# Preparing the last attention's first pair inside the first attention, in a two-layer fp32 kernel on one core

## The chip, the cores and the metric

The kernel runs on one core of a Trainium2 chip. Its time is the device time of one execution in microseconds, and the median of three runs is taken. TensorE (PE) multiplies matrices, VectorE (DVE), ScalarE (ACT) and GpSimd (POOL) work on rows, SyncE (SP) issues most transfers. Each engine runs its own queue of instructions in order and waits on semaphores for the others.

## The reference

Four stages in turn are added to x, of 4 batches, 512 tokens and 256 channels, all in fp32:

```python
x = x + _L0_attn_ref(_layernorm(x, axis=-1), ...)   # linear attention
x = x + _L0_ffn_ref(_layernorm(x, axis=-1), ...)    # Hadamard FFN
x = x + _L1_attn_ref(_layernorm(x, axis=-1), ...)   # "first attention" below
x = x + _L1_ffn_ref(_layernorm(x, axis=-1), ...)    # "last attention" and experts
```

`_L1_attn_ref` is softmax attention over 16 query heads and 4 key/value heads of 16 channels, with rotated queries and keys. `_L1_ffn_ref` starts with another attention, causal, and ends with a mixture of experts:

```python
h = _rms(x, ln_w)
q = (h @ wq).reshape(B, S, NHEADS, HEAD_DIM)      # 32 heads of 64
k = (h @ wk).reshape(B, S, KVHEADS, HEAD_DIM)     # 8 heads
v = (h @ wv).reshape(B, S, KVHEADS, HEAD_DIM)
q, k = _rope(q, k)
...
x = x + o @ wo
h = _rms(x, ff_ln_w)
...
return x + moe
```

Here x enters already as a layer norm of the residual, so each token has two factors: `zinv`, the layer norm's inverse root of the variance, and `hinv`, that of the RMS norm on top of it, both worked out from the token's mean and variance `mvs`.

## The kernel before, in words

Tokens are cut in tiles of 128, four to a batch (`NT`); `xt[i]` holds one tile of the residual. The order of the instructions on each engine is written by hand (`manual_schedule`): the order of the Python calls is the order in the queues. Four stages follow each other: the linear attention, the FFN (which also makes keys and queries of the first attention for batches 0 and 1), the first attention, the last attention with routing and experts.

**The first attention** (from L940) is one loop of 66 steps, 16 to a batch: step `i` of batch `b` is head group `j = i // 4` and token tile `t = i % 4`. A step issues, in this order:

- `row_fill1` for the next batch: four score matmuls (L329) and four row maxima on DVE (L335). In batch 3 there is no next batch, so these are missing;
- at `i = 0`, `maxima1` (L977, L980) and `complete1`; at every other step one piece from the list `fill1` (`extra1`); at `t = 2` another `complete1` (POOL, L962, L965, L967), which makes the shifted query and key of the next head group;
- `normalise1` (ACT L1020 and L1021, four POOL operations L1022 to L1025) at `i = 2, 6, 10, 14`, for the head group finished before;
- `col_fill1`: four transposed score matmuls (L989) and four exponentials on ACT (L995);
- `weigh1` (L1002) for the step before and, after a group's last tile, `sums1` (ACT copy L1012, DVE shuffle L1014).

The pieces of `fill1` are queries and values of the next batch, the four token tiles of the previous batch's out-projection (`out_proj1`: eight matmuls of L234, the DVE add L1031 and the statistics L1033 and L1034, which fill `mvs`) from step 5, and `fresh1`, rows, transposes, keys and queries of the batch after next. PSUM is a ring of seven banks beside one for the weighed sums.

**The seam** between the two attentions: after the loop come the last `normalise1` and the four `out_proj1` of batch 3. Then `inv_root_log` works out the norms of all 16 token tiles at once, twice (L210 to L218, L1093 to L1098): a DVE scale and shift, Ln and Exp on ACT, one Newton step on DVE. With `zinv` and `hinv` there, `fresh(0)` normalises the rows of batch 0 (`norm_rows`, four POOL operations, L1149) and transposes them (`turn`, L1170; ACT leaves by L1176).

**The last attention** runs by pairs of units. A unit is eight query heads, made in two blocks of `q_lo` and `q_hi`, and two key/value heads; a pair of units shares `keys_lo`, `keys_hi` (both in `rope_half`: four matmuls L225, an ACT copy L1190, two POOL multiplications L1193 for a low half, four operations L1199 and L1200 for a high half) and `values` (L234, ACT copy L1251, eight transfers to DRAM L1257). `twice` copies keys to both halves of the partitions (SP, L1234), `spread` brings values back from DRAM in another layout (SP, L1271), and `normed` makes the rows `z` of the new residual (POOL, L1160). `q_hi` also orders the next query weights (`fetch_q`, SP, L1207). For the first pair all of that is issued ahead of the loop. Then a loop of five steps to a unit issues score fills (`fill`, L1298), DVE minima with the causal mask (`least`, L1316), exponentials (L1328), DVE transposes (L1345), weighing (L1375) and out-projections with `wo4` (L1425). In it a list `soon` holds work that is dealt out by the step, with "pause" entries that end a step's share. The weight `wo4` (2 MB) is loaded with the others ahead of the first attention.

Of the kernel before, what the change touches and what calls it, by code (L numbers as in the profile page):

```python
# [10 lines left out]
F32 = mybir.dt.float32  # L11
# [78 lines left out]
def kernel(  # L90
# [172 lines left out]
    def rows_of(b):  # L263
        tiles = []
        for t in range(NT):
            i = b * NT + t
            xn = piece_tile([P, D], "xn1", 4)
            nc.gpsimd.tensor_scalar(
                xn, xt[i], amv[:, i, 0:1], ainv[:, i : i + 1],
                ALU.subtract, ALU.mult,  # L270
            )
            tiles.append(xn)
        xnTs[b] = piece_tile([P, KC, S], "xnT1", 2)
        return tiles
# [63 lines left out]
    with ExitStack() as l0:  # L338
# [352 lines left out]
        with ExitStack() as f0:  # L691
# [5 lines left out]
            made1 = {}  # L697

            def outliving(shape, tag, bufs):
                if tag[:2] in ("qp", "kr", "kz"):  # L700
                    made1[tag] = made1.get(tag, -1) + 1
                    return wp5.tile(
                        shape, F32, tag=f"{tag}_{made1[tag]}", bufs=1, name=tag
                    )
                return fp.tile(shape, F32, tag=tag, bufs=bufs, name=tag)

            where["tile"] = outliving
# [180 lines left out]
    wo4 = wp4.tile([P, 16, D], F32, tag="wo4", name="wo4")  # L888
# [7 lines left out]
    nc.sync.dma_start(out=wo4, in_=w_o4)  # L896
# [38 lines left out]

    banks.close()
# [5 lines left out]
    with ExitStack() as a1:  # L942
        a1.enter_context(tc.manual_schedule())
        with tc.issue_after(latest["root"].ins):
# [7 lines left out]
        where["tile"] = lambda shape, tag, bufs: ap1.tile(  # L952
            shape, F32, tag=tag, bufs=bufs, name=tag
        )
# [96 lines left out]
        last = held = None  # L1051
        for k in range(4 * NT * B + 2):
# [4 lines left out]
            if i == 3 and 1 < b + 1 < B:  # L1057
                fill1.append(lambda b=b: values1(b + 1))
            if i == 5 and 0 < b <= B:
                fill1.extend([lambda t=t, b=b: out_proj1(b - 1, t) for t in range(NT)])  # L1060
            if i == 5 and b + 2 < B:
                fill1.extend(fresh1(b + 2))
            if b + 1 < B:
                row_fill1(b + 1, j, t)
# [7 lines left out]
            if held is not None:  # L1072
                normalise1(*held)
                held = None
# [5 lines left out]
            if last is not None:  # L1080
                weigh1(*last)
                if last[2] == NT - 1:
                    held = last[:2] + sums1(*last[:2])
            last = at + (pT,) if pT is not None else None
        normalise1(*held)
        assert not fill1
        for t in range(NT):
            out_proj1(B - 1, t)

        inv = inv_root_log(mvs[:, :, 1], EPS_LN, B * NT)
        nc.vector.tensor_copy(zinv, inv)  # L1093
        msq = stat.tile([P, B * NT], F32, tag="msq", name="msq")
        nc.vector.tensor_tensor(msq, zinv, zinv, ALU.mult)
        nc.vector.tensor_tensor(msq, msq, mvs[:, :, 1], ALU.mult)
        inv = inv_root_log(msq, EPS_RMS, B * NT)
        nc.vector.tensor_tensor(hinv, inv, zinv, ALU.mult)  # L1098
# [10 lines left out]
    with ExitStack() as a2:  # L1109
# [3 lines left out]
        units = []  # L1113
# [5 lines left out]

        def unit(name):  # L1120
            pool, bufs = units[-1]
            return pool.tile([P, 512], F32, tag="u", bufs=bufs, name=name)

        NU = 4 * B
        hTs, zs, krs, vsrs, qrs, lots, pend = ({} for _ in range(7))
        scores, probs, turned, heaps, wides, rsb, oTs, vds = ({} for _ in range(8))


        held = []
        putting_off = [False]  # L1130

        def drain(fn):
            if putting_off[0]:
                held.append(fn)
            else:
                fn()

        def drain_one():
            if held:
                held.pop(0)()  # L1140


        def norm_rows(b):
            hTs[b] = ap2.tile([P, KC, S], F32, tag="hT", bufs=2, name="hT")
            hn = []
            for t in range(NT):
                i = b * NT + t
                h = rp.tile([P, D], F32, tag="hn", bufs=4, name="hn")
                nc.gpsimd.tensor_scalar(  # L1149
                    h, xt[i], mvs[:, i, 0:1], hinv[:, i : i + 1],  # L1150
                    ALU.subtract, ALU.mult,
                )
                hn.append(h)
            return hn
# [9 lines left out]

        def turn(dst, col, srcs, scale):

            pt = unit("pt").rearrange("p (c n) -> p c n", c=KC)
            for i, src in enumerate(srcs):
                for c in range(KC):
                    nc.tensor.transpose(  # L1170
                        pt[:, c, i * P : (i + 1) * P], src[:, c * P : (c + 1) * P], ident
                    )

            def leave():
                for c in range(KC):
                    nc.scalar.activation(  # L1176
                        dst[:, c, col : col + 2 * P], pt[:, c, :], AF.Copy,
                        scale=scale[:, c : c + 1],
                    )

            drain(leave)

        def rope_half(dst, half, w, at, hT, scale):

            pr = unit("pr")
            project(pr, w, slice(at, at + P), hT, slice(0, S))

            def leave():
                raw = ap2.tile([P, S], F32, tag="raw4", bufs=2, name="raw4")
                nc.scalar.activation(raw, pr, AF.Copy, scale=scale)  # L1190
                if half == 0:
                    for i, name in enumerate(("cos4", "sin4")):
                        nc.gpsimd.tensor_tensor(dst[:, i, :], raw, R(name), ALU.mult)  # L1193
                    return
                for i, (name, op) in enumerate(
                    (("sin4", ALU.subtract), ("cos4", ALU.add))
                ):
                    part = ap2.tile([P, S], F32, tag="part4", bufs=1, name="part4")
                    nc.gpsimd.tensor_tensor(part, raw, R(name), ALU.mult)  # L1199
                    nc.gpsimd.tensor_tensor(dst[:, i, :], dst[:, i, :], part, op)  # L1200

            drain(leave)

        def fetch_q(k):
            if k < 2 * NU:
                wqs[k] = wp4.tile([P, KC, 2 * P], F32, tag="wq4", bufs=3, name="wq4")
                nc.sync.dma_start(out=wqs[k], in_=w_q4[k % 8])  # L1207

        def q_lo(k):
            if k >= 2 * NU:  # L1210
                return
            qrs[k] = ap2.tile([P, 2, S], F32, tag="qr4", bufs=4, name="qr4")
            rope_half(qrs[k], 0, wqs[k], 0, hTs[k // 8], 1.0)

        def q_hi(k):
            if k >= 2 * NU:
                return
            rope_half(qrs[k], 1, wqs.pop(k), P, hTs[k // 8], 1.0)
            fetch_q(k + 3)


        def keys_lo(q):
            pend[q] = ap2.tile([P, 2, S], F32, tag="krq", bufs=1, name="krq")
            rope_half(pend[q], 0, wk4, 256 * (q % 2), hTs[q // 2], -0.125)

        def keys_hi(q):
            rope_half(pend[q], 1, wk4, 256 * (q % 2) + P, hTs[q // 2], -0.125)

        def twice(u):

            kr = ap2.tile([P, 2, S], F32, tag="kr4", bufs=2, name="kr4")
            part = slice(64 * (u % 2), 64 * (u % 2) + 64)
            for i in range(2):
                nc.sync.dma_start(  # L1234
                    out=kr[64 * i : 64 * i + 64, :, :], in_=pend[u // 2][part, :, :]
                )
            krs[u] = kr

        def values(q, half):
            if half == 0:  # L1240
                pend["v"] = ap2.tile([P, NT, 256], F32, tag="vs4", bufs=1, name="vs4")
            pv = unit("pv4").rearrange("p (t n) -> p t n", t=2)
            for i in range(2):
                project_tok(
                    pv[:, i, :], hTs[q // 2], tok(2 * half + i), wv4,
                    slice(256 * (q % 2), 256 * (q % 2) + 256),
                )
            vs = pend["v"]

            def leave():  # L1250
                nc.scalar.copy(vs[:, 2 * half : 2 * half + 2, :], pv)  # L1251
                if half == 1:

                    vd = dram.tile([2, 32, 16, P], F32, tag="vd", bufs=2, name="vd")
                    for p2 in range(2):
                        for cc in range(4):
                            nc.sync.dma_start(  # L1257
                                out=vd[p2, :, cc:16:4, :],
                                in_=vs[rows(cc), :, P * p2 : P * p2 + P],
                            )  # L1260
# [993 lines left out]
```

## Time and profile before

| | us |
|---|---|
| median of three runs | 1767.79 (1761.07 to 1770.71) |
| the profiled execution | 1779.78 |
| its span | 1777.9 |
| busy in the span: PE | 1624.5 (91%) |
| DVE | 1002.4 (56%) |
| ACT | 825.5 (46%) |
| POOL | 894.5 (50%) |

The mean granted clock over the span is 0.966. Times in the text below are microseconds from the start of the span of this execution. The profile's groups give, for each line, the number of instructions, their mean duration, and what ended the idle time ahead of them; the records in time order give a start, a busy time, the engine, line and operation, the output and inputs with their shapes, and in brackets the idle time before and its releaser. The busy shares are means over stages with different limits, and the stages are read apart below.

### The profile page before, as it was taken

To read this page: it belongs to the slowest core of one execution; us is meant where nothing else is said; L and a number is where in the kernel's file an instruction comes from. 1 tells how busy PE (TensorE), PEld (TensorE's weight loads), DVE (VectorE), ACT (ScalarE), POOL (GpSimd) and SP (SyncE) were. 2 spreads that over 40 slices of the span, in tenths; PEclk is the share of its full clock that TensorE was granted. 3 is DMA by queue.
4 is the path that set the end of the run, shared out by engine and by line. 5 is a ranking of instruction groups with operands and counts; after the bars stand their busy time and mean duration, and the time that the engine had idled before them with its cause. 6 is when DMAs were issued, how large, how long until landed. Compare 5 with 4: busy or idle time off the path is not lost.

```text
span 1777.9 us, 42123 instructions
## 1 busy us (share of the span) xinstructions
PE 1624.5 (91%) x16100; PEld 950.4 (53%) x16100; DVE 1002.4 (56%) x3069; ACT 825.5 (46%) x2162; POOL 894.5 (50%) x914
## 2 busy tenths in 40 slices
PE   7999999999999986899999999999989868899993
PEld 4665554553334223466666666666666635455552
DVE  4547336556666412667766686668756924433333
ACT  4431122125655762566666665666556514233331
POOL 3224133225565545755466647794667244844442
PEclk9999999999999997899999999999999979899997
DMA  9992000020000001322222222322222037655556
GB/s 348 371 369 84 0 1 0 1 102 1 1 1 1 1 1 43 77 55 56 56 56 55 56 56 56 87 75 59 61 61 68 6 122 235 154 97 87 86 88 167
DMA packets 106934, 146.59 MB, mean 82 GB/s; under 512 B 11632, under 2 KB 86128, under 8 KB 106352
## 3 DMA queue, kind: packets, MB, share of 16 engines
q1 hardware_dynamic: 91856, 123.54, 22.9%
q0 software_dynamic: 14448, 19.80, 6.5%
q8 instruction: 131, 2.15, 0.5%
q14 instruction: 67, 0.55, 0.1%
q10 hardware_dynamic: 432, 0.55, 0.1%
HBM read 67.17 MB, written 68.29 MB: 76 GB/s over the span
## 4 chain that ended last, share of the span: by engine, by line
PE 41%; POOL 5%; issue 5%; ACT 5%; DVE 4%; DMA 1%; SPq 0%; another core or an unknown queue 0%; ACTq 0%; DVEq 0%; POOLq 0%
PE po L1375 9%; PE ph L1947 8%; PE sc L1298 6%; PE py L1425 5%; PE pr L225 4%; PE pyx L1947 3%; ACT masked L1328 2%; PE pq L1403 1%; POOL xs L1612 1%; POOL part L1199 1%; DVE masked L1316 1%; ACT raw L1190 1%; PE ptx L1983 1%; PE pa L2016 1%; POOL qr L1200 1%
## 5 line engine op out<-in xcount | busy, mean ns | idle before, releaser
L1328 ACT ACTIVATE masked<-masked,mx 128x256 f32<-128x256 f32 (+3 forms) x512 | 281.1, 553 | 4.8 <-DVE mx L1316 4.8
L1316 DVE CUSTOM_DVE_ANT_0 masked<-sc,cst 128x256 f32<-128x256 f32 (+3 forms) x512 | 214.0, 481 | 44.6 <-PE sc L1298 44.5
L1375 PE MATMUL po<-pT,vsr 32*64 32x128 f32 (+1 forms) x8064 | 198.1, 289 | 39.6 <-issue 24.9
L1375 PEld LDWEIGHTS po<-pT,vsr 32*64 32x64 f32 x8064 | 158.3, 132 | 90.0 <-issue 41.8
L1345 DVE STREAM_TRANSPOSE pT<-masked 128x512 f32<-128x512 f32 x256 | 168.5, 691 | 57.7 <-ACT masked L1328 57.2
L2029 POOL DMA_INDIRECT acc<-yx,goes x79 | 123.2, 1559 | 138.9 <-ACT yx L2028 101.4
L335 DVE TENSOR_REDUCE top<-sc 128x1 f32<-128x512 f32 x256 | 158.7, 682 | 56.3 <-PE sc L329 56.3
L1298 PE MATMUL sc<-kr,qr 32*128 32x128 f32 (+3 forms) x2048 | 173.9, 460 | 10.8 <-POOL qr L1200 3.7
L1947 PE MATMUL ph<-wall,hTx 128*128 x316 | 163.5, 641 | 11.6 <-DVE hTx L1985 6.9
L995 ACT ACTIVATE pT<-sT 128x512 f32<-128x512 f32 x256 | 131.5, 604 | 60.8 <-PE sT L989 60.6
L1434 POOL TENSOR_TENSOR z<-z,y 128x256 f32<-128x256 f32 x64 | 47.3, 740 | 195.9 <-ACT y L1433 195.8
L1415 DVE TENSOR_TENSOR oT<-po,rsb 128x128 f32<-128x128 f32 x256 | 61.3, 287 | 139.4 <-PE po L1375 127.1
L2009 DVE TENSOR_TENSOR ax<-ph,gx 128x256 f32<-128x256 f32 x79 | 33.6, 425 | 166.2 <-ACT gx L2007 154.7
L1425 PE MATMUL py<-wo,oT 128*128 128x256 f32 x512 | 123.7, 390 | 2.3 <-DVE oT L1415 1.6
L1199 POOL TENSOR_TENSOR part<-raw,rtab 128x512 f32<-128x512 f32 x80 | 102.5, 1281 | 43.1 <-ACT raw L1190 39.8
L1298 PEld LDWEIGHTS sc<-kr,qr 32*128 32x128 f32 x2048 | 90.5, 189 | 60.5 <-issue 29.0
L225 PE MATMUL pr<-hT,wq 128*128 128x512 f32 x256 | 122.0, 601 | 0.0
L225 PE MATMUL pgu<-xnT,wug 128*128 128x512 f32 x256 | 114.5, 598 | 1.5 <-DVE xnT L190 1.5
L989 PE MATMUL sT<-qr,km 32*128 32x512 f32 x512 | 108.1, 634 | 7.0 <-POOL km L967 2.8
L1425 PEld LDWEIGHTS py<-wo,oT 128*128 128x128 f32 x512 | 94.6, 192 | 31.2 <-DVE pT L1345 7.6
L1406 ACT COPY rsb<-pq 128x512 f32<-128x512 f32 x64 | 36.0, 587 | 134.8 <-PE pq L1403 129.7
L1947 PEld LDWEIGHTS ph<-wall,hTx 128*128 128x128 f32 x316 | 55.8, 196 | 79.1 <-issue 43.2
(301 smaller groups left out, 2884.9 us busy)
## 6 DMA issues: line engine op xcount, KB each, us to landing
xs<-zero SPq DMA_DIRECT2D x16, 2304.0 KB
vsr<-vd SPq DMA_DIRECT2D x256, 64.0 KB
wall<-in_w_exp_dram SPq DMA_DIRECT2D x16, 768.0 KB
xin<-xs SPq DMA_DIRECT2D x79, 144.0 KB
wq<-in_w_q_dram SPq DMA_DIRECT2D x33, 256.0 KB
kr<-krq SPq DMA_DIRECT2D x32, 256.0 KB
acc<-zero SPq DMA_DIRECT2D x2, 2176.0 KB
vd<-vs SPq DMA_DIRECT2D x64, 64.0 KB
```

The source lines that it names most:

```text
L225: nc.tensor.matmul(dst, lhsT=w[:, c, cols], rhs=srcT[:, c, tok], start=(c == 0), stop=(c == n - 1),)
L335: nc.vector.tensor_reduce(top[:, at : at + 1], sc, AX.X, ALU.max)
L995: nc.scalar.activation(pT[:, g, :], us[g], AF.Exp)
L1199: nc.gpsimd.tensor_tensor(part, raw, R(name), ALU.mult)
L1298: nc.tensor.matmul(scs[s][:, at : at + w], lhsT=qrs[2 * u + jj][rows(s), ab, tok(t)], rhs=krs[u][rows(s), ab, :w], start=(ab == 0), stop=( ...
L1316: nc.vector.tensor_tensor_reduce(masked[:, part], sc[:, part], C("cmask")[:, S - (t + 1) * P :], 1.0, 3e38, ALU.add, ALU.min, mx[:, t, i : ...
L1328: nc.scalar.activation(part, part, AF.Exp, bias=lots[u, "mx"][:, t, i : i + 1], scale=-1.0, accum_out=lots[u, "sm"][:, t, i : i + 1],)
L1345: nc.vector.transpose(dst[:, 2 * (f % 2) + s // 2, :], p)
L1375: nc.tensor.matmul(heaps[u, phase][a][64 * g : 64 * g + 64, first * P : last * P], lhsT=vsrs[u][rows(a), c, 64 * g : 64 * g + 64], rhs=src ...
L1425: nc.tensor.matmul(py[:, :D], lhsT=oT[:, j, :], rhs=wo4[:, 4 * (u % 4) + j, :], start=(j == 0), stop=(j == 3),)
L1947: ins = nc.tensor.matmul(out, lhsT=lhsT, rhs=wall[:, bass.ds(w_at[i] + at, n)], **kw)
L2029: nc.gpsimd.indirect_dma_start(out=accs[i % 2][:, :], out_offset=bass.IndirectOffsetOnAxis(ap=goes[:, i : i + 1], axis=0), in_=y[:, :], in ...
```

## The change

1. The helpers of the last attention (`unit`, `norm_rows`, `turn`, `rope_half`, `q_lo`, `q_hi`, `keys_lo`, `keys_hi`, `twice`, `values`) are defined ahead of the first attention, and their tiles come from a new pool `w_first` (transposed rows and query tiles alternate between it and the old pool).
2. `first_pair`, a list of ten pieces, holds what was the preparation of the first pair. Seven are put into `fill1` at step 1 of batch 3, ahead of the out-projection of batch 2, which so moves from steps 5 to 8 to steps 8 to 11. The other three run behind the last `normalise1`, ahead of batch 3's out-projection.
3. `inv_root_log` at the seam is replaced by `norms(b, n)`, three pieces for `n` batches from `b`. Batch 0's are put into `fill1` in batch 1 and come at its steps 13 to 15, batch 1's in batch 2 at steps 9 to 11, those of batches 2 and 3 together in `soon`, in the last attention's steps 1 to 3. `norm_rows(0)` runs at step 12 of batch 2.
4. `wo4` becomes a tile of the last attention's pool and is loaded behind the first unit's `spread`; `normed(0)` goes into `soon`, at step 0.
5. To make room, the transposed rows `xnT1` have one buffer in place of two, and queries and keys of the first attention share one ring from the FFN on (`place_in`).

The core of the diff:

```diff
+    def norms(b, n):
+        part = slice(b * NT, (b + n) * NT)
+        st = {}
+
+        def begin(var, eps):
+            st["v"] = stat.tile([P, n * NT], F32, tag="rn_v", name="rn_v")
+            nc.vector.tensor_scalar(st["v"], var, 1.0, eps, ALU.mult, ALU.add)
+            st["y"] = stat.tile([P, n * NT], F32, tag="rn_y", name="rn_y")
+            nc.scalar.activation(st["y"], st["v"], AF.Ln)
+            nc.scalar.activation(st["y"], st["y"], AF.Exp, scale=-0.5)
+
+        def end():
+            y, r = st["y"], stat.tile([P, n * NT], F32, tag="rn_r", name="rn_r")
+            nc.vector.tensor_tensor(r, y, y, ALU.mult)
+            nc.vector.tensor_tensor(r, r, st["v"], ALU.mult)
+            nc.vector.tensor_scalar(r, r, -0.5, 1.5, ALU.mult, ALU.add)
+            nc.vector.tensor_tensor(r, r, y, ALU.mult)
+            return r
+
+        def second():
+            nc.vector.tensor_copy(zinv[:, part], end())
+            msq = stat.tile([P, n * NT], F32, tag="rn_m", name="rn_m")
+            nc.vector.tensor_tensor(msq, zinv[:, part], zinv[:, part], ALU.mult)
+            nc.vector.tensor_tensor(msq, msq, mvs[:, part, 1], ALU.mult)
+            begin(msq, EPS_RMS)
+
+        return [
+            lambda: begin(mvs[:, part, 1], EPS_LN),
+            second,
+            lambda: nc.vector.tensor_tensor(hinv[:, part], end(), zinv[:, part], ALU.mult),
+        ]
...
+        first_pair = [
+            lambda: turn(hTs[0], 0, hn1[:2], SM("ln_w")),
+            lambda: turn(hTs[0], 2 * P, hn1[2:], SM("ln_w")),
+            lambda: keys_lo(0),
+            lambda: (keys_hi(0), twice(0), twice(1)),
+            lambda: q_lo(0),
+            lambda: q_hi(0),
+            lambda: q_lo(1),
+            lambda: q_hi(1),
+            lambda: values(0, 0),
+            lambda: values(0, 1),
+        ]
...
+            if i == 1 and b == B - 1:
+                fill1.extend(first_pair[:7])
             if i == 5 and 0 < b <= B:
                 fill1.extend([lambda t=t, b=b: out_proj1(b - 1, t) for t in range(NT)])
             if i == 5 and b + 2 < B:
                 fill1.extend(fresh1(b + 2))
+            if i == 5 and 0 < b < B - 1:
+                fill1.extend(norms(b - 1, 1))
+            if i == 12 and b == B - 2:
+                fill1.append(lambda: hn1.extend(norm_rows(0)))
...
+        for piece in first_pair[7:]:
+            piece()
         for t in range(NT):
             out_proj1(B - 1, t)
-
-        inv = inv_root_log(mvs[:, :, 1], EPS_LN, B * NT)
...
-        start = fresh(0)
-        for _, piece in start:
-            piece()
-        keys_lo(0)
...
-        for a in range(4):
-            spread(0, a)
-        normed(0)
+        for i in range(4):
+            spread(0, i)
+        nc.sync.dma_start(out=wo4, in_=w_o4)
+        soon.append((False, lambda: normed(0)))
+        for piece in norms(2, 2):
+            soon += [(False, piece), ("pause", lambda: None)]
```

## The prediction

> **What bounds the kernel now.** I read the busy time by stretches first, then the chain that ended last, then the records in time order around the place where the first attention gives way to the last one (the seam). By stretches; columns are length, busy PE, PEld, DVE, ACT, POOL (with instruction counts), granted clock, DMA share, GB/s:
>
> ```profile
> 603.00:659.00 56.00, 51.93 (x326) 16.63 (x326) 7.82 (x22) 43.64 (x85) 32.28 (x29) 1.00 0.00 1
> 659.00:704.00 45.00, 28.81 (x84) 17.47 (x88) 7.33 (x28) 7.37 (x16) 21.96 (x19) 0.81 0.10 23
> 704.00:745.00 41.00, 32.34 (x391) 15.69 (x383) 25.14 (x88) 24.83 (x77) 35.65 (x29) 0.83 0.35 84
> ...
> 790.00:834.00 44.00, 41.52 (x753) 27.29 (x743) 30.43 (x109) 26.69 (x82) 27.94 (x25) 1.00 0.23 61
> ```
>
> Before 659 and after 745 PE is busy over nine tenths at clock 1.00. Between, in the seam (659 to 704) and the last attention's first unit, PE idles a quarter of the time, its clock falls, and POOL is busiest. The chain says which POOL work:
>
> ```profile
> 685.39 5.45 issue
> 690.84 2.49 POOL krq L1193 x2
> ...
> 712.73 1.27 POOL qr L1200
> 714.00 0.04 issue
> 714.04 2.09 PE sc L1298 x8
> ```
>
> From 690.84 to 714.0 the path is POOL's rotations of keys and queries, one after another. The seam in time order:
>
> ```profile
> 665.17 1.26 POOL L1025 TENSOR_TENSOR aoT<-raw,sums 128x512 f32<-128x512 f32 x1
> ...
> 666.49 8.82 PE L234 MATMUL py<-wo,aoT 128*128 128x256 f32 x26 [6.03 <-POOL aoT L1025]
> ...
> 676.48 0.17 DVE L210 TENSOR_SCALAR rt_v<-mvs 128x16 f32<-128x16 f32 x1
> 676.69 0.22 ACT L212 ACTIVATE rt_y<-rt_v 128x16 f32<-128x16 f32 x1 [14.87 <-DVE rt_v L210]
> ...
> 680.55 4.83 POOL L1149 TENSOR_SCALAR hn<-x,mvs,hinv 128x256 f32<-128x256 f32 x4 [14.12 <-DVE hinv L1098]
> ...
> 686.68 5.10 PE L225 MATMUL pr<-hT,wk 128*128 128x512 f32 x8 [0.56 <-ACT hT L1176]
> ...
> 703.65 1.14 PE L1298 MATMUL sc<-kr,qr 32*128 32x512 f32 x8 [1.54 <-POOL qr L1200]
> ```
>
> It is a serial string: normalise, out-projection, norms of all tokens, four rows, transposes, projections, rotations, first scores. And one step of batch 2, where norm pieces will be put:
>
> ```profile
> 597.37 2.46 DVE L335 TENSOR_REDUCE top<-sc 128x1 f32<-128x512 f32 x4
> 597.50 0.63 ACT L1020 ACTIVATE r<-sums 128x512 f32<-128x512 f32 x1 [0.89 <-DVE sums L1014]
> ...
> 598.16 0.63 ACT L1021 ACTIVATE r<-r 128x512 f32<-128x512 f32 x1
> 598.70 2.04 ACT L995 ACTIVATE pT<-sT 128x512 f32<-128x512 f32 x4
> ```
>
> DVE spends 2.5 us of each 4 us step on the maxima; ACT spends 2.05 on four exponentials.
>
> **The change part by part** (span time; negative is saved).
>
> (a) The seam. Before, the last weigh ends at 658.96 and the first score fill starts at 703.65: 44.7 us. After, rows, transposes, keys and three query halves are already done. What is left: normalise until 666.43 (7.5); the out-projection's 26 recorded matmuls, 8 of which took 1.99 at clock 1.00 (622.72), so 6.5; the last token tile's add, 0.5. Score fill starts 14.5 after the weigh instead of 44.7. The second query half (four matmuls, 1.9) and the values (sixteen, 3.6) run inside the 6.03 us that PE idled. Fill 0 newly waits for the last add and the values' copy; on PE everything stands behind it, and both are in the 14.5. **-30.1**. Bounds: -27.7 if the out-projection keeps its 8.82 at the low clock; -30.5 if the add overlaps.
>
> (b) The first unit. Score fills 0, 1, 2 of the first unit start at 703.65, 711.35, 721.76: 18.1 us from fill 0 to 2, waiting on POOL's rotations, which after the change are done or three halves ahead. By the other engines' rows two fills need: fill matmuls 2.0, two projection groups of 1.9, DVE minima 2.5 and transposes 2.5 in part beside them: 9.6. **-8.5**. Bounds: -10.3 (7.8, two steps without the minima) and -0.5 (two steps at the later stages' mean, 44/5 = 8.8 each). I take the near end, as these first fills carry no weighing yet.
>
> (c) Batch 3 takes seven pieces and pushes the out-projection of batch 2 from steps 5-8 to 8-11. Steps 1 to 3 have PE waiting (0.90 for km at 607.72; 0.5 and 0.56 for ACT at 611.5 and 614.2), which takes the two turns and the first key half: 0. Steps 4 to 11 then each have 4.0 us of PE (a score group 1.07, a weigh 1.0, a rope half 1.9; an out-projection step 618.72 to 622.72 is 4.0 too), 32.0 against 27.0 for 616.66 to 643.63 now. **+5.1**. Bounds: 0, and +10.7 if all moved PE work is added (5 groups of 1.9, 2 turns of 0.6). POOL takes 17.7 of rotations (a first half 2.5, a second 5.1; three and two of them) onto 32.3 of 56: 50, under the stretch, but by this order the query of head group 2 is complete at about 637.2 where it is needed at 638.9: cover of 1.7 us. The four key transfers of `twice` go onto SP, idle there (1 GB/s).
>
> (d) Norms in batches 1 and 2, three pieces each. Both queues, DVE and ACT, run in order. First piece: `rn_v` stands behind four maxima, so ends 3.8 after the step's score matmuls start (583.99: maxima end 587.63, plus 0.18); Ln and Exp of the norm (0.22 + 0.21) end at 4.35; the four exponentials queued behind them start at 4.35 instead of 2.0. Their lateness passes to the raw copy, its shuffle, the next maxima: **+2.3**. Second piece, in a step with a normalise: eight DVE operations at a spacing of 0.21 (rows 676.48 on) are 1.7, then norm Ln/Exp 0.5, normalise's Ln/Exp 1.2, four exponentials 2.05, then scores 1.1 and a weigh 1.0: 7.6 from maxima's end to the score matmuls two groups on, against 4.3 now (583.67 to 587.94): **+3.3**. Third: five DVE operations, 1.05, in the 1.5 that DVE idles each step: 0. Together 5.7 a batch, **+11.4** for two. Bounds: 0 (the path takes it up) and +13.3 (the third piece too on the path, 6.65 a batch). Four `norm_rows` on POOL (4.83) in batch 2 stand beside POOL's idle (11.58 before 598.87): 0; without cover 4.8.
>
> (e) Norms of batches 2 and 3 in the first unit's steps 1 to 3: the middle piece's eight DVE operations, 1.7, where DVE is dense (726 to 734): **+1.7**, bounds 0 and 3.
>
> (f) The rest at 0. The 2 MB of `wo4` now goes out behind the first unit's spread; 2 MB was moved in about 4.7 us at 389.4 before, and the first out-projection reads it some six steps later (35 us); the second unit's spread and the query weights stand behind it on SP and have that cover too; without it 4.7. The spread's transfers, now issued right behind the values, are read some 16 us later. Shared rings and the one `xnT1` buffer: the instruction order shows no new wait in batches 0 to 2.
>
> A rule that speaks against (d), to be weighed. The Trainium skill, "TensorE: Matmul & The Clock Gate", section "What's actually happening", has PE's clock halve after an idle window of about 3.4 us. A stalled second piece leaves PE about 3 us in two stretches: by the rule no window is idle throughout, and nothing is added.
>
> The row here is 3.15 us of idle at 711.35, after which four matmuls at 716.07 took 3.78 where 1.88 is usual. By that row each of two stalls could add 1.9, +4 in all; I take 0, the stall being split, and keep +4 for the range.
>
> Sum: -30.1 - 8.5 + 5.1 + 11.4 + 1.7 = **-20.4**, span 1777.9 to 1757.5. The later stages are PE-bound (41.5 of 44 in 790 to 834), so the shift carries to the end. The profiled execution took 1779.8 and is 12 above the median of the runs, 1767.8, which I shift: **1747**.
>
> **The rivals.**
> Forecast: -20.4, 1747; its own range 1740 to 1757 by (c) and (d) between their bounds.
> R1, norms hidden: DVE's 1.5 idle per step takes the pieces and the chain absorbs ACT's lateness. For: ACT is busy only 43.6 of 56 in batch 3. Against: ACT's queue is strictly ordered, and the exponentials stand behind `rn_v`. -31.8: 1736.
> R3, the last batch doesn't take the work: all moved PE work adds, 10.7, and a query comes late by a stall of 2.3 as in (d), (c) = +13: 1755. For: 51.93 of 56 PE busy already. Against: 50 of POOL in 61.
> R4, given back in the first unit: POOL's rotations for the next unit and keys (three pairs of 2.5 and 5.1, 22.8), `z` 4.8 and rows 4.8 fill 32.5 of 33.7 us, so (b) is lost: 1756. For: POOL is 35.65 of 41 there. Against: three of its halves have left.
> R2, the slower side: the norm pieces chain in ACT's and DVE's queues so that each of nine costs a whole step, 4.3, 38.7 in place of (d) and (e): -33.5 + 38.7 = +5.2, 1773; with 1.9 for a fallen clock at each, +22, 1790. It decides from 3.7 us a piece. For: a late exponential makes maxima late, and these the next piece. Against: a third piece has no ACT work at all.
> Also, the change could not do what it says; the instruction order shows the pieces where they are said to be.
>
> **How the numbers follow.** Forecast 0.44, R1 0.14, R3 0.16, R4 0.10, R2 0.16. A measurement of this kernel can tell about 0.5% (8.8 us) from no change: 1759.0 and 1776.6. Faster: forecast, R1, six tenths of R3 and R4: 0.74. Same: the rest of these, a third of R2: 0.16. Slower: two thirds of R2: 0.10. Range: from R1 less 3, 1733, to R4 and part of R2, 1767.
>
> **What would show it.** (a) the first fill some 14.5 after the last weigh, PE clock near 1.00 through the seam. (b) fill 2 within 10 of fill 0. (c) steps of 4.0 in batch 3, POOL busy near 50. (d) ACT idle ended by `rn_v` in batches 1 and 2, batch 2 longer by 5.7. (e) first unit's minima late by the middle piece. It is wrong if steps with a norm piece lengthen by over 3.7, if fill 0 still waits for POOL, or if later stages lengthen.

## The result, and the profile after

The changed kernel takes 1755.1 us, the median of 20 runs (1744.8 to 1762.3), against 1766.8 for the kernel before (20 runs, 1759.0 to 1775.3). The ratio is 0.993, with a 95% interval of 0.9916 to 0.9944: some 12 us (0.7%) faster, where 20.4 were forecast.

The profiled executions mislead here. Their spans are 1777.9 and 1757.6, 20.3 apart and next to the forecast's 1757.5, but the profiled execution of before was slower than any of its 20 timed runs. Followed through the two traces, the changed kernel is 9.6 us ahead when the last attention's second unit begins and 9.9 ahead at its thirteenth unit (1228.86 against 1238.74); the other 10 come behind that, in the last units and the routing, which the change doesn't touch. There two executions of the changed kernel itself differ by more: 528.8 us to the end in this one, 545.6 in the run e10_changed below. So the shift to explain is the first one, of about 10 us, which agrees with the medians.

Both kernels cut at the same events, in stretches of busy time; the columns are those of the prediction (stretch, length, busy PE, PEld, DVE, ACT, POOL with counts, granted clock, DMA share, GB/s). The stretches are batches 1, 2 and 3 of the first attention, the seam from the last weigh's end to the first score fill, and from there to the second unit's first minima. Before:

```profile
455.69:532.07 76.38, 75.48 (x460) 28.75 (x457) 51.09 (x93) 44.10 (x84) 47.37 (x40) 1.00 0.00 1
532.07:604.09 72.02, 70.70 (x436) 26.76 (x432) 47.75 (x87) 41.83 (x80) 33.47 (x30) 1.00 0.00 1
604.09:658.96 54.87, 50.80 (x321) 16.43 (x317) 7.04 (x20) 42.55 (x83) 31.20 (x28) 1.00 0.00 1
658.96:703.65 44.69, 28.50 (x82) 17.21 (x81) 7.33 (x28) 7.37 (x16) 21.64 (x18) 0.81 0.09 20
703.65:747.60 43.95, 34.48 (x402) 16.70 (x404) 27.69 (x96) 24.83 (x77) 38.50 (x32) 0.84 0.37 91
```

After:

```profile
454.04:539.40 85.36, 82.85 (x460) 31.75 (x457) 54.68 (x107) 44.59 (x88) 47.42 (x40) 0.92 0.00 1
539.40:619.88 80.48, 78.51 (x437) 29.59 (x433) 51.01 (x101) 42.32 (x84) 38.30 (x34) 0.92 0.00 1
619.88:679.84 59.96, 58.50 (x349) 19.92 (x345) 7.02 (x20) 46.88 (x92) 48.68 (x42) 1.00 0.10 23
679.84:693.84 14.00, 12.55 (x54) 9.68 (x53) 4.34 (x13) 3.50 (x6) 9.87 (x9) 1.00 0.24 57
693.84:738.00 44.16, 37.95 (x404) 19.50 (x404) 34.25 (x113) 24.16 (x78) 28.97 (x24) 0.88 0.38 112
```

The seam is 30.7 shorter and batch 3 is 5.1 longer, as forecast. Batches 1 and 2 are 9.0 and 8.5 longer (5.7 each were forecast), and the first unit has gained nothing (6.8 were forecast for (b) and (e) together). In batch 1 PE has the same 460 recorded matmuls and is busy 7.4 us longer, at a mean clock of 0.92 where it was 1.00: most of the lengthening is PE at a slower clock.

How a norm piece gets there, in the records in time order of the changed kernel, batch 1. The first piece is issued at 522.44, the middle one from 528.5 on:

```profile
522.44 0.16 DVE L1087 TENSOR_SCALAR rn_v<-mvs 128x4 f32<-128x4 f32 x1
522.63 0.20 ACT L1089 ACTIVATE rn_y<-rn_v 128x4 f32<-128x4 f32 x1 [2.60 <-DVE rn_v L1087]
...
526.88 1.12 PE L1164 MATMUL sT<-qr,km 32*128 32x512 f32 x2 [0.69 <-DVE top L335]
...
529.91 0.17 DVE L1087 TENSOR_SCALAR rn_v<-rn_m 128x4 f32<-128x4 f32 x1
530.12 0.20 ACT L1089 ACTIVATE rn_y<-rn_v 128x4 f32<-128x4 f32 x1 [4.62 <-DVE rn_v L1087]
...
531.64 2.04 ACT L1170 ACTIVATE pT<-sT 128x512 f32<-128x512 f32 x4
531.81 1.26 POOL L1197 TENSOR_TENSOR sums<-sums,r 128x512 f32<-128x512 f32 x1 [10.20 <-ACT r L1196]
532.28 1.22 PE L329 MATMUL sc<-kz,qp 32*128 32x512 f32 x1 [1.04 <-ACT pT L1170]
...
535.98 1.94 PE L1177 MATMUL oT<-pT,v 128*32 128x512 f32 x8
```

At the first piece ACT idles 2.60 us until DVE's `rn_v`; the exponentials, the raw copy, its shuffle and the maxima follow late, and PE waits 0.69 for the maxima. At the middle piece ACT idles 4.62 us, with the exponentials queued behind `rn_v`, and PE then waits 1.04 for them. This is the mechanism of step (d). But the weigh at 535.98 takes 1.94 for eight matmuls that take 1.06 elsewhere. The trace's record of the granted clock has PE at half from 528.6 for 10.2 us, and again from 593.5 for 10.2 at the same place of batch 2. Each covers a norm's middle piece but starts with its first operations or ahead of them (528.53 and 594.40): what stands ahead of the fall is PE's pause behind the first piece, 0.69 us here and 0.78 in batch 2.

Two short stretches at half clock, 3.4 us at 467.2 and at 552.5, lie at no norm piece. The kernel before met none in these batches, yet it has the same pause ahead of them, 10.9 us into each batch. Batch 1 of before, then of after:

```profile
467.34 1.12 PE L989 MATMUL sT<-qr,km 32*128 32x512 f32 x2 [0.79 <-DVE top L335]
```

```profile
465.69 1.12 PE L1164 MATMUL sT<-qr,km 32*128 32x512 f32 x2 [0.79 <-DVE top L335]
```

So these two stretches can't be put down to the norm pieces.

In the first unit, the chain of waits:

```profile
693.84 2.09 PE sc L1352 x16
...
696.82 4.83 PE sc L1352 x16
701.64 5.89 PE pr L225 x8
...
715.03 1.14 DVE rn_r L1096
...
716.20 0.18 DVE rn_r L1097
...
716.40 1.14 DVE zinv L1101
```

POOL has left it. In its place stand a second fill of 4.83 (before the change such sixteen matmuls took 2.0 at full clock), projections at half clock, and then the norm's DVE operations, two of them 1.14 us long where their neighbours take 0.18.

### The profile page after: what moved, and what is told of

Same layout as the page of the kernel before. It is cut to its first block, busy times and chain, and to the rows that moved or that the text cites. A ratio compares the mean times of both kernels' runs of the same rounds, so it can differ in the third digit from the quotient of the medians.

```text
span 1757.6 us, 42136 instructions
## 1 busy us (share of the span) xinstructions
PE 1626.2 (93%) x16100; PEld 952.7 (54%) x16100; DVE 1011.9 (58%) x3097; ACT 826.7 (47%) x2170; POOL 895.9 (51%) x914
## 4 chain that ended last, share of the span: by engine, by line
PE 75%; DVE 7%; ACT 6%; POOL 5%; issue 4%; DMA 2%; SPq 0%; DVEq 0%; ACTq 0%; POOLq 0%
PE ph L1991 8%; PE po L1429 8%; PE sc L1352 7%; PE pgu L225 6%; PE py L1479 6%; PE py L234 6%; PE pr L225 5%; PE sT L1164 5%; PE sc L329 4%; PE pyx L1991 4%; PE oT L1177 3%; PE pq L225 2%; ACT masked L1382 2%; PE pv L234 2%; PE pq L1457 1%
## 5 line engine op out<-in xcount | busy, mean ns | idle before, releaser
L1382 ACT ACTIVATE masked<-masked,mx 128x256 f32<-128x256 f32 (+3 forms) x512 | 281.1, 553 | 13.6 <-DVE mx L1370 13.6
L1429 PE MATMUL po<-pT,vsr 32*64 32x128 f32 (+1 forms) x8064 | 186.6, 286 | 31.0 <-issue 16.0
L1429 PEld LDWEIGHTS po<-pT,vsr 32*64 32x64 f32 x8064 | 153.3, 131 | 75.1 <-issue 26.8
L1352 PE MATMUL sc<-kr,qr 32*128 32x128 f32 (+3 forms) x2048 | 180.8, 467 | 7.0 <-DVE mx L1370 4.4
L1352 PEld LDWEIGHTS sc<-kr,qr 32*128 32x128 f32 x2048 | 95.0, 194 | 58.7 <-issue 32.2
L1006 POOL TENSOR_TENSOR qr<-raw,rtab 128x512 f32<-128x512 f32 x64 | 80.9, 1286 | 33.1 <-ACT raw L1003 33.1
L1382 ACT ACTIVATION_READ_ACCUMULATOR masked<-masked,mx 128x1 f32 x512 | 97.6, 191 | 0.0
```

Source lines behind the costliest of these rows:

```text
L1352: nc.tensor.matmul(scs[s][:, at : at + w], lhsT=qrs[2 * u + jj][rows(s), ab, tok(t)], rhs=krs[u][rows(s), ab, :w], start=(ab == 0), stop=( ...
L1382: nc.scalar.activation(part, part, AF.Exp, bias=lots[u, "mx"][:, t, i : i + 1], scale=-1.0, accum_out=lots[u, "sm"][:, t, i : i + 1],)
L1429: nc.tensor.matmul(heaps[u, phase][a][64 * g : 64 * g + 64, first * P : last * P], lhsT=vsrs[u][rows(a), c, 64 * g : 64 * g + 64], rhs=src ...
```

## The experiments

The runs below were timed on two chips on which the kernel before takes 1786 to 1791, so ratios to it are given. Half clock is a granted clock of 0.5 in the trace's record. A stretch's loss to it is worked out as half of what PE is busy at half clock; the rest is called its length at full clock. That is an estimate, good to about 1 us: batch 2 of the changed kernel comes out at 73.7 in one execution and 74.9 in another.

| kernel | ratio (95%) | batch 1, us (lost to half clock) | batch 2 | first unit |
|---|---|---|---|---|
| before | 1 | 76.4 (0) | 72.0 (0) | 44.0 (5.0) |
| changed | 0.993 (0.9916 to 0.9944) | 85.4 (6.3) | 80.5 (6.8) | 44.2 (5.1) |
| e10_changed, the same again | 0.994 (0.990 to 0.997) | 84.0 (4.4) | 80.0 (5.1) | 43.9 (6.4) |
| e1_split | 0.985 (0.979 to 0.992) | 81.2 (5.1) | 72.0 (0) | 43.7 (5.1) |
| e2_late | 0.990 (0.985 to 0.995) | 85.3 (6.4) | 80.5 (6.8) | 39.4 (3.4) |
| e3_batch2 | 0.991 (0.988 to 0.995) | 83.9 (4.5) | 73.6 (1.7) | 40.3 (1.7) |
| e4_firstsplit | 0.989 (0.985 to 0.994) | 78.9 (0) | 76.9 (5.1) | 41.7 (3.4) |
| e5_both | 0.980 (0.975 to 0.985) | 81.2 (5.1) | 72.0 (0) | 41.0 (5.1) |
| e6_pairlate | 1.003 (1.000 to 1.006) | 88.8 (8.5) | 84.1 (9.9) | 40.0 (1.7) |
| e7_busy | 0.993 (0.991 to 0.996) | 86.3 (0) | 81.8 (0) | 43.6 (3.4) |
| e8_qearly | 0.978 (0.973 to 0.983) | 78.0 (1.7) | 72.0 (0) | 34.5 (0) |
| e11_best, e8 again | 0.979 (0.974 to 0.983) | 76.4 (0) | 72.0 (0) | 38.1 (3.4) |

**e1_split: the ACT part of a norm one step after its DVE part.** For the batches of the first attention `norms` returns five pieces:

```diff
         def begin(var, eps):
             st["v"] = stat.tile([P, n * NT], F32, tag="rn_v", name="rn_v")
             nc.vector.tensor_scalar(st["v"], var, 1.0, eps, ALU.mult, ALU.add)
+
+        def root():
             st["y"] = stat.tile([P, n * NT], F32, tag="rn_y", name="rn_y")
...
+            return [
+                lambda: begin(mvs[:, part, 1], EPS_LN), root, second, root,
+                lambda: nc.vector.tensor_tensor(hinv[:, part], end(), zinv[:, part], ALU.mult),
+            ]
```

> The norms of batches 0 and 1 are cut in five pieces in place of three: each Ln/Exp pair on ACT is issued one step after the DVE operations it reads, so ACT's queue never stands behind fresh DVE work. Nothing else is changed. Theory (ACT's exponentials wait behind a norm's Ln, which waits behind the maxima on DVE): batch 1 from 85.4 us to 77 to 78, batch 2 from 80.5 to 72 to 74, the stretches of half clock near 529 and 594 gone, last weigh at 664 to 667 in place of 679.8, time about 14 below the changed kernel, near 1741. Rival A (shared rings, one xnT1 buffer, POOL rows lengthen the batches): 85 and 80 stay. Rival B (the DVE operations themselves are the price): under 2 us shorter each, since their number is the same.

Batch 2 is 72.01 us, as in the kernel before, with all the norm operations in it, and the half clock of batches 1 and 2 at the norm pieces is gone. Batch 1 is 81.2, not 77 to 78: it met a half clock of 10.2 us at 468.1, before any norm is issued; without its 5.1 us it is 76.1, as before the change (the last two of its five pieces run in the first steps of batch 2). The ratio, 0.985, times 1766.8 is 1741. Records in time order:

```profile
526.01 0.16 DVE L1087 TENSOR_SCALAR rn_v<-mvs 128x4 f32<-128x4 f32 x1
...
526.54 0.58 ACT L1194 COPY raw<-oT 128x512 f32<-128x512 f32 x1
527.02 0.21 ACT L1091 ACTIVATE rn_y<-rn_v 128x4 f32<-128x4 f32 x1
...
527.16 0.72 DVE L1196 STREAM_SHUFFLE sums<-raw 128x512 f32<-128x512 f32 x1
```

`rn_v` is written at 526.0 and read by ACT at 527.0 behind the raw copy; nothing waits for it. Rival A (rings, buffers) and rival B (the number of DVE operations) are out: both are unchanged here. The busy time of DVE in batch 2 even rose, 52.1 us against 51.0, in a batch 8.5 shorter.

**e2_late: the norms of batches 2 and 3 in the third unit.**

```diff
-        for piece in norms(2, 2):
-            soon += [(False, piece), ("pause", lambda: None)]
...
+            if n == 10:
+                for piece in norms(2, 2):
+                    soon += [(False, piece), ("pause", lambda: None)]
```

> The norms of batches 2 and 3 are moved from the last attention's steps 1 to 3 to steps 10 to 12 (third unit). Theory (their DVE operations stand between minima and transposes where DVE is the bound, and wait for POOL's operations): first fill to the second unit's first minima from 44.2 us to 37 to 40, the third unit longer by 0 to 3, time about 4 below the changed kernel, near 1751. Rival (POOL's rotations, rows and z bound the first unit): stays within 1 us of 44.2, and the time within 1.

The first unit is 39.4, 4.8 shorter, of which 1.7 is half clock not met; the second unit and the third, which now holds the norms, take 46.6 and 43.7, against 47.1 and 44.5, so no more is paid back than 1.2 us (the second unit of the changed kernel is 45.4 at full clock). With POOL's work unchanged, its rotations didn't hold the unit at 44.2: the rival R4 of the prediction is out as a mechanism.

**e3_batch2: no norm pieces in batch 2.** They join those of the first unit (`norms(1, 3)`); the rows of batch 0 stay in batch 2.

> The norms of batch 1 are taken out of batch 2's steps and done with those of batches 2 and 3 in the last attention's steps 1 to 3, so batch 2 has no norm pieces and keeps the rows of batch 0 on POOL. Theory (norm pieces lengthen the batches): batch 2 from 80.5 us to 72 to 73, batch 1 stays at 85, first unit within 1.5 of 44.2, time about 8 below the changed kernel, near 1747. Rival A (rows on POOL, shared rings, one xnT1 buffer): batch 2 stays near 80.

Batch 2 falls from 80.5 to 73.6, with 1.7 lost to a half clock met at 553.7; without it 71.9, as before. So `norm_rows` on POOL costs nothing that shows here. The first unit was expected to stay; it fell to 40.3, since it met half clock for 3.4 us in place of 6.8 and 3.4: at full clock it is 38.6, against 39.0. The ratio puts the kernel some 4 us below the changed one, with an interval that takes in the 8 expected.

**e4_firstsplit: only the first piece cut.**

> Only the first piece of the norms in batches 1 and 2 is cut (its Ln/Exp comes a step later); the middle piece stays whole. By the prediction's terms (2.3 for the first piece, 3.3 and the fallen clock for the middle one): batch 1 from 85.4 us to 82 to 83, batch 2 from 80.5 to 77.5 to 78.5, the stretches of half clock stay, time about 5 below the changed kernel, near 1750. If the first piece starts the whole chain of late work: both batches near 77 and 73, no half clock, as with all pieces cut.

Half right. Batch 1 is 78.9 at clock 1.00 throughout, which the prediction's terms didn't foresee; batch 2 is 76.9 with 5.1 lost to half clock. The cut also moves the middle piece a step on, out of the normalise step, so against the changed kernel the two pieces are not told apart. Against e1_split they are: both have the first piece cut, and only here is the middle piece whole. PE pauses 1.38 and 1.39 us for the exponentials behind it, and the clock falls behind both pauses, at 533.2 for 3.4 us and at 591.2 for 6.8; in e1_split neither is there. So each piece can bring the clock down by itself: in the changed kernel the first one did, here the middle one. Batch 1 escapes because it ends at 531.94, before the fall. Busy time by batch:

```profile
453.07:531.94 78.87, 76.59 (x461) 29.03 (x457) 54.52 (x105) 44.35 (x88) 47.41 (x40) 1.00 0.00 1
531.94:608.83 76.89, 74.90 (x434) 27.73 (x433) 48.96 (x103) 42.93 (x85) 38.28 (x34) 0.93 0.00 1
```

With nearly the same work in batch 1, PE is busy 76.6 us at clock 1.00 here, and 82.9 at 0.92 in the changed kernel: 6.3 apart, which is what the half clock was reckoned to cost.

**e7_busy: more work for PE beside the norm pieces.** Four matmuls that nothing reads are added to each of the six steps.

```diff
+        def more():
+            if n == 1:
+                dm = unit1("dm")
+                for _ in range(4):
+                    nc.tensor.matmul(dm, lhsT=ident, rhs=rtab3[:, 0, :], start=True, stop=True)
```

> The changed kernel with four matmuls more (128x512, 1.9 us, read by nothing) on PE in each of the six steps of batches 1 and 2 that carry a norm piece. Theory (most of what the norm pieces cost is PE's halved clock, which a stalled step brings on): no half clock near 529 and 594, batch 1 from 85.4 us to 79 to 83, batch 2 from 80.5 to 75 to 78, though PE has 11.4 us more to do. Rival (the price is the stall on ACT alone, the clock adds nothing): the batches stay or grow by up to 6 each.

Inconclusive. No half clock is left in either batch, which speaks for PE's pauses as what brings it on (the longest near the norm pieces are 0.5 and 0.6 us here), though the pause 10.9 us into each batch stands here too and the clock stayed up behind it. But the batches didn't get shorter: 86.3 and 81.8. The three groups added 5.7 us to a batch, which all came onto the path (79.1 for the changed batch 1 at full clock and 5.7 make 84.8; 1.5 is left over): they take a bank of the ring, and so wait where the scores wait. The lengths fit the rival's numbers, and this run can't say how the cost is shared. The spread over executions can: in five runs batch 1 carries the same norm pieces, and 85.4, 84.0, 85.3, 83.9 and 88.8 become 79.1, 79.6, 78.9, 79.4 and 80.4 once half clock is taken off, beside e4's 78.9 which had none.

**e6_pairlate: the seven pieces back behind the loop.**

```diff
             if i == 1 and b == B - 1:
-                fill1.extend(first_pair[:7])
+                pass
...
-        for piece in first_pair[7:]:
+        for piece in first_pair:
```

> The seven pieces of the first pair are moved out of batch 3 to behind the loop, in front of the three that are there already; norms and rows stay ahead. Theory (batch 3 hides POOL's rotations behind PE work): batch 3 from 60.0 us to 55, last weigh to first fill from 14.0 to 23 to 26, first unit 44 to 48, time 4 to 10 above the changed kernel. Rival (batch 3 is bound by PE, so nothing is hidden there): batch 3 shorter by what the seam and the unit grow, time within 2 of the changed kernel.

Batch 3 is back at 54.9, and the seam grows to 27.4 (23 to 26 expected); the first unit, expected at 44 to 48, is 40.0. In all 4.1 us more than in the changed kernel; 5.8 at full clock. So batch 3 does hide POOL's rotations, for about that much. The time was expected 4 to 10 us above the changed kernel; the ratio's rise, from 0.993 to 1.003, is some 18, and with 1.000 to 1.006 the kernel is about as slow as the one before. The profiled execution lost 5.3 us more to half clock in batches 1 and 2 and 14 more behind the first unit, but it is one execution, and why the median of ten rose by that much is not shown.

**e5_both and e8_qearly: a version that beats both.** e5 cuts all norms in five and moves the last ones to step 10. e8 adds one line, so that PE has work between the first two fills:

```diff
-                if f == 1:
+                if f == (1 if u else 0):
                     q_lo(2 * u + 2)
```

> All norms in five pieces, those of batches 2 and 3 from step 10 of the last attention on. Theory (norm pieces cost a stall and a fallen clock wherever their ACT part follows fresh DVE work): batch 1 at 76.4 plus what half clock it meets (up to 5), batch 2 at 72.0, first unit 39 to 40, second unit's first minima 22 to 29 earlier than in the kernel before; time 10 to 15 below the changed kernel, 0.979 to 0.986 of the kernel before. Rival (the gains of the two parts overlap): no better than the better one alone, 0.985 to 0.99.

> The kernel with both parts, and the low half of the third query block is issued in step 0 of the first unit in place of step 1, where PE waits between the first two fills for the minima. Theory (the first unit's clock falls because PE waits there): no half clock near the first unit's second fill, first unit 1 to 4 us shorter than with both parts alone. Rival (the unit is bound by DVE minima and transposes): first unit within 1 us.

e5 is at 0.980; its first unit is 41.0, a little over the 39 to 40 expected, with 5.1 lost to half clock. e8's first unit is 34.5 with none: 6.5 shorter, over the 1 to 4 expected. The busy time in it, and PE's records in time order:

```profile
677.10:711.59 34.49, 32.38 (x404) 17.49 (x404) 28.32 (x98) 23.23 (x74) 28.51 (x23) 1.00 0.46 141
```

```profile
677.10 2.00 PE L1358 MATMUL sc<-kr,qr 32*128 32x512 f32 x16 [0.56 <-issue]
679.02 1.98 PE L225 MATMUL pr<-hT,wq 128*128 128x512 f32 x4
680.94 2.86 PE L1358 MATMUL sc<-kr,qr 32*128 32x512 f32 x16
683.73 1.98 PE L225 MATMUL pr<-hT,wk 128*128 128x512 f32 x4
685.90 3.83 PE L1358 MATMUL sc<-kr,qr 32*128 32x128 f32 x32 [0.19 <-DVE mx L1376]
```

The projection at 679.02 stands where PE waited for the minima to free the score banks; the second fill takes 2.86 in place of 4.83, and the third starts 8.8 us after the first, where it was 13.6. At full clock e8 gains 1.4 on e5 (34.5 against 35.9), the other 5.1 is the clock.

**e10_changed and e11_best: the changed kernel and e8 on one chip.**

> The changed kernel itself, beside the next one and the kernel before on one chip. Theory: 0.988 to 0.996 of the kernel before; batch 1 at 79 and batch 2 at 73.7 us once the time lost to half clock is taken off, whatever half clock this execution meets.

> The kernel with norms in five pieces, the last ones late, and the early query half, again. Theory: 0.974 to 0.983 of the kernel before, faster than the changed kernel by 10 to 20 us on the same chip; batch 1 near 76.2 and batch 2 near 72.0 once half clock is taken off, first unit near 34.5. Rival (its time was a lucky run of clock): 0.984 or more.

1776.5 and 1749.3 us, with the kernel before at 1785.7. They are 27 us apart, over the 10 to 20 expected. e11 met 3.4 us of loss in the first unit (38.1; 34.7 at full clock), so that part of e8's gain there was luck: with the second fill fed the clock can still fall, here at 687.7 and 701.3, behind the second fill. But the ratio held: 0.979, against 0.994. In e10 batch 2 is 74.9 at full clock, 1.2 over the 73.7 expected.

## Why the prediction came out as it did

(a) The seam: right. 30.7 against 30.1; the out-projection's 26 matmuls ran in 5.88, at full clock, and the values and the last query half filled PE's pause.

(c) Batch 3: right, 5.1 against 5.1. Its steps run at 4.0 us, POOL is busy 48.7 (50 forecast), and no wait for a late query appears, so R3 is out.

(d) The norms in batches 1 and 2: the mechanism was right, the sum was not. Of 17.4 us, 4.4 is the stall (2.7 and 1.7 at full clock; 6.1 together in e10_changed), where 11.4 was forecast, and 13.1 is PE's clock, put at 0. Of that, 9.7 lies in the two stretches behind the first pieces, and 3.4 in the two short ones, behind a pause that the kernel before has too: the latter is no price of the norms. The stall too large and the clock left out are errors against each other, so the term looks better than its working was. The step that failed is the sentence "I take 0, the stall being split". It followed the page's rule that an idle window of about 3.4 us lowers the clock; here it fell without one. In the 3.4 us ahead of the falls at 528.6 and 593.5 PE was busy 2.7 and 2.6, and its longest pause was 0.7 and 0.8 us.

The row at 716.07, which the prediction set beside the rule, was misread: the record of the clock has PE at half from 706.6 for 13.7 us, so from before the 3.15 us of idle, and what stood ahead of that fall were pauses of 1.54 us. It pointed the right way, but "+4 in all" was too little as well, since the clock stayed down for 10.2 us at each place, not for four matmuls. The Trainium skill, "TensorE: Matmul & The Clock Gate", also has a section "A second HAM failure mode: psum-queue depth-cycling", which tells of a bf16 kernel whose short idle times between groups of matmuls come often enough to make the clock fall and rise. These traces, of fp32 matmuls and with one pause in the 3.4 us ahead of a fall, are nearer to that section than to the window rule as it was used.

As the records read, the 2.3 and 3.3 of the stall were too large together because a late exponential isn't late for everything: PE had a weigh and next scores to do, and only pauses of 0.7 to 1.0 us came through.

(b) The first unit: off by size. POOL no longer sets it, as forecast, but from the first to the third fill it took 13.6, not 9.6. The sum left out that the second fill waits for the minima to free its banks one by one (PE paused 0.98 us for them ahead of 696.82), and the half clock behind it, from 699.3 for 6.8 us. With these fills fed (e8) it takes 8.8. The kernel before had shown this wait. Its record of the second fill's first half:

```profile
711.35 2.09 PE L1298 MATMUL sc<-kr,qr 32*128 32x512 f32 x8 [3.15 <-DVE pT L1345]
```

The 3.15 us of idle ended with DVE's work, not with POOL's, where the prediction read all three fills as waiting for POOL's rotations.

(e) The norms in the first unit: 4.8 with a short half clock, 3.1 without, where 1.7 was forecast. DVE's operations there are longer than the rows they were priced by. The two long ones beside POOL's work, in the changed kernel:

```profile
714.86 1.28 POOL L1012 TENSOR_TENSOR part<-raw,rtab 128x512 f32<-128x512 f32 x1
715.03 1.13 DVE L1096 TENSOR_SCALAR rn_r<-rn_r 128x8 f32<-128x8 f32 x1
716.21 1.28 POOL L1013 TENSOR_TENSOR qr<-qr,part 128x512 f32<-128x512 f32 x1
716.40 1.13 DVE L1101 COPY zinv<-rn_r 128x8 f32<-128x8 f32 x1
```

Each ends with POOL's operation. Six of the 14 norm operations there are held like this, for some 4.5 us in all by their length over the usual 0.17; that the hold is the cause of the 3.1 was not tried by itself.

(f) held: no wait for `wo4`, for the spread or for a ring appears.

Sum at the second unit's first minima: -1.7 up to batch 1 (the spread of executions), +9.0 + 8.5 + 5.1 - 30.7 + 0.2 = -9.6. Against -20.4, (d) is short by 6.0 and (b) with (e) by 7.0; the rest goes 2.2 the other way. That the two profiled spans are 20.3 apart, as forecast, is luck.

The measured time, 1755.1, is that of R3 and R4 (1755 and 1756), and neither is its cause: batch 3 took its work as forecast, and what R4 saw given back in the first unit was given back to DVE's minima and norm work and to the clock, not to POOL. R1 (norms hidden) is what e1 reaches in batch 2 by the order of issue; the change itself doesn't. R2 (each piece a whole step of 4.3) would have needed 38.7 for nine pieces; six took 17.4 at most and the three in the first unit 3 to 5. It was right that the pieces cost more than their work, and wrong on the reason.

## What to carry to other kernels

An operation that hops from one in-order engine to another and back is better issued with its second part a step behind the first: here the same instructions then cost nothing, where issued together they cost 4 to 6 us of stall and some 10 of clock. A pause on a nearly full PE has to be priced with the clock it may bring down: here a pause under 1 us cost up to 5 us behind it, and whether it does depends on the execution (e10_changed kept full clock behind the pause that cost the changed kernel the stretch at 467.2), so lengths are compared after half clock is taken off. Two profiled spans are not the result: follow the shift from event to event, and see where executions of one kernel part.

## What was not expected of the hardware

- In batches 1 and 2 of the changed kernel PE's clock fell behind pauses of 0.7 and 0.8 us, in stretches of 3.4 or 10.2 us; in e11_best's first unit it fell where PE paused for no more than 0.41 us at a time in the 3.4 us ahead. The kernel before kept full clock behind the 3.4 us from 611.0, in which PE was busy only 2.4. Nor does steady work bring the clock back at once: in e1_split PE is busy through all of the 10.2 us at half from 468.1.
- The same pause of 0.79 us, 10.9 us into batch 1, stands in all twelve profiled executions, and the clock fell behind it in six of them. Within an execution the falls lie whole multiples of 3.41 us apart. On that grid the six pauses that began 0.4 to 1.7 us into a stretch of 3.41 us were followed by half clock from the next stretch on, and the six that began 1.9 to 2.5 us into one were not. This was read from the records and not tried; other pauses don't all fit (in batch 2 two that began 1.9 and 2.0 us in were followed by half clock), so what decides is not settled.
- A DVE operation of 128x4 or 128x8 that starts while POOL runs a two-input operation is mostly held until that ends. In the changed kernel, of 42 such operations the 26 that started with POOL idle took 0.15 to 0.17 us; of the 10 that started inside a POOL two-input operation, 8 were held, up to 1.2 us, and all 8 ended within 0.03 us of its end. It was seen in the records, and not tried by an experiment of its own.
